# Where the weight sums of a Winograd feed-forward are made: in its first group, or by pieces in the stages before it

## The chip, the cores and the metric

The kernel runs on one core of a Trainium2 chip. The metric is the time of one execution on the device, in microseconds (us). Engines are named as the profile names them: PE is TensorE (with PEld, its weight loads), DVE is VectorE, ACT is ScalarE, POOL is GpSimd, SP is SyncE, which here only issues DMAs.

## What is computed

Two transformer layers over x of shape (2, 1024, 512) in float32. Each of four blocks is normed ahead and behind, and added to x:

```
x = x + ln(attention0(ln(x)))    # each token on its own: softmax of q.k over 8 heads of a group
x = x + ln(ffn0(ln(x)))          # ternary weights, hidden 1408, sigmoid gate
x = x + ln(attention1(ln(x)))    # 16 heads, 4 key/value heads, causal, rotary
x = x + ln(ffn1(ln(x)))          # hidden 2048
ffn1: h = silu(x @ w_gate) * (x @ w_up)
      of every 4 neighbours of h keep the 2 largest by size, the rest become 0
      return h @ w_down
```

The change concerns mostly `ffn1`, the last stage.

## The kernel before

The 2048 tokens are 16 tiles of 128, taken in 4 groups of 4 tiles; x stays in SBUF (`x_sb`). The stages follow each other: attention 0 with the loads, the first feed-forward (113 to 400 us, with the projections of the second attention's first tiles in its last group), the second attention (to 960 us), the last feed-forward (from 960.75 us).

**First feed-forward.** For each group and each of 11 hidden blocks `l0_hidden` (L365) multiplies (L371), gates, and splits the hidden tile in a rounded part and the rest; the rest is made on POOL (L380). `l0_out` (L385) multiplies both by the third weight two to three steps later (L390). A group's end adds the normed output to x on POOL (L411); the first block's output of the next group is added on POOL too (L300).

**Second attention.** It is a list of 96 steps (`t_steps`, L978), 16 tasks (batch, half of the queries, key head) in turn. A step (`prob_step`, L816) computes transposed scores for one block of keys, takes the exponential on ACT, and, on the diagonal, zeroes what lies ahead with `affine_select` on POOL (L838). `value_step` (L845) follows two steps later. Meanwhile `score_step` (L738) finds the row maxima (L758, DVE) and sums (L762, ACT) of later tasks, `shifts` (L796) turns them to logarithms on DVE, and a table `due` holds pieces of other work by step: `later` (L897) puts a function at a step. Through it go the projections of batch 1 (`project_parts`, L454: norm and transpose; project and rotate, with two adds on POOL at L520; transpose back, split and store to DRAM), the output tiles (`output_parts`, L862: multiply, norm, add to x on POOL at L876), and at the end the first work of the last stage (`f1_begin`, L1053).

**Last feed-forward.** Its products are made by Winograd's form of 2 x 2 block multiplication: seven products, for which each operand needs four sums of its blocks. A unit of weights (gate or up: eight units, two tiles each) has four raw blocks of 128 x 256 values, and the same in each of the four groups. `derive` (L927) makes the four sums on POOL, `load_unit` (L905) loads a unit two ahead. In group 0 a unit is loaded raw, derived, and its seven blocks' last four are kept in DRAM (`kept`); later groups load three raw blocks and four kept ones. Units 0 and 1 are derived within the attention, the others in group 0. The down weights (four parts `S`) go the same way (`load_down` L1116, `derive_down` L1130): parts 0 and 1 on POOL, 2 and 3 on DVE, the sums kept from group 0 on. A group has a hidden half (`f1_unit`, L1168, products at L1160, additions at L1166, gate products at L1221 and L1222, the choice of 2 of 4 at L1255 and L1280) and a down half (`f1_down`, L1305, products at L1315). `f1_collect` (L1321) adds the product sums of a pair of tiles, `f1_store` (L1359) norms them and adds them to x. The reciprocal root for the norm is made on DVE by 13 small operations (`inverse_root`, L182), save for the last pair, where ACT takes the square root (L177).

**Who sets the order.** `tc.manual_schedule(engines=...)` names the engines whose order is that of the program text. From L543 on and from L973 on that is PE alone; the order of DVE, ACT, POOL and SP is made by a planner with costs of its own. The last feed-forward (L1425) has all five engines in the order of the text. [...]

Of the kernel before, what the change touches and what calls it, by code (L numbers as in the profile page):

```python
# [18 lines left out]
P = 128  # L19
GT = 4  # L20
# [4 lines left out]
def two_layer_sandwich(  # L25
# [386 lines left out]


    NH, NKV, DK = 16, 4, 32
    REP = NH // NKV
# [33 lines left out]
    def a1_stats(st, G):  # L449
        tiles = [x_sb[:, st.b * TB + G * GT + k, :] for k in range(GT)]  # L450
        mv, rs = ln_stats(aw, tiles, f"a1_{st.b}_{G}", roots=False)
        st.ln[G] = mv, rs, minus_mean(aw, mv, rs, GT)

    def project_parts(st, i, on_act=False):  # L454
# [30 lines left out]
        def second():  # L485
# [20 lines left out]
            for h0, n, ps_qk, ct, sit, rb_h in (  # L506
                (NH, NKV, pkv, cos_t, sin_t, rbs[0]), (0, NH, pq, cosq_t, sinq_t, rbs[1])
            ):
                src = ps_qk[:, : n * DK].rearrange("p (h f) -> p h f", f=DK)
                ra_h = h.ra[:, h0 : h0 + n, :]  # L510
                nc.vector.tensor_tensor(
                    ra_h, src, ct[:, i, :].unsqueeze(1).to_broadcast([P, n, DK]), ALU.mult
                )
                half = [P, n, DK // 2]
                for par in range(2):
                    nc.vector.tensor_tensor(
                        rb_h[:, :, par::2], src[:, :, 1 - par :: 2],
                        sit[:, i, par::2].unsqueeze(1).to_broadcast(half), ALU.mult,
                    )
                nc.gpsimd.tensor_tensor(ra_h, ra_h, rb_h, ALU.add)  # L520

        def third():
            pq, pk = bank[0](f"pqT_{nm}"), bank[0](f"pkT_{nm}")
            ra = h.ra.rearrange("p h f -> p (h f)")
# [17 lines left out]

    with tc.manual_schedule(engines={mybir.EngineType.PE}):  # L543
        l0_stats(0, range(1))
# [67 lines left out]
        for g in range(NG):  # L612
            nxt = None
            for hc in range(HC):
# [28 lines left out]
                else:  # L643
# [5 lines left out]
                    if 1 <= hc <= 2 * GT:  # L649
                        if hc % 2:  # L650
                            parts[hc // 2][0]()
                            if hc > 1:
                                parts[hc // 2 - 1][2]()
                        else:
                            parts[hc // 2 - 1][1]()
                    elif hc == 2 * GT + 1:
                        parts[GT - 1][2]()
                        done[0] = GT
                        parts[GT][0]()
                if g == NG - 2 and hc == 4:  # L660
                    p0_stack.close()
# [200 lines left out]
    def output_parts(st, Q):  # L862

        def part(ii):
# [10 lines left out]
            ln_apply(tmp, py, mv, rs, 0)  # L875
            nc.gpsimd.tensor_tensor(xt, xt, tmp, ALU.add)  # L876

        return [lambda ii=ii: part(ii) for ii in range(GT)]

    P5_BUFS = 1  # L880
    dw = ctx.enter_context(
        tc.tile_pool(name="dw", bufs=FF // P, space=bass.MemoryType.DRAM)
    )

# [16 lines left out]
    w1a = None  # L901
    NU = FF // (2 * P)
    raw, derived, kept = {}, {}, {}

    def load_unit(n):  # L905


        res = []
        for i, src in enumerate((f1_wg, f1_wu)):
            pool = w1b if n % 3 == 2 else w1a  # L910
            w = pool.tile(
                [P, 7, 2, P], F32, tag="w7", name=f"w7_{n}_{i}", bufs=2 if n % 3 == 2 else 4
            )
            if n < NU:
                nc.sync.dma_start(out=w[:, 0:4].rearrange("p b c m -> p (b c m)"), in_=src[n])
            else:
                nc.sync.dma_start(
                    out=w[:, 0:3].rearrange("p b c m -> p (b c m)"), in_=src[n % NU][:, : 6 * P]
                )
                nc.sync.dma_start(out=w[:, 3:7], in_=kept[n % NU, i])  # L920
            res.append(w)
        if n < NU:
            raw[n] = res
        else:
            derived[n] = [[w[:, k] for k in range(7)] for w in res]

    def derive(n):  # L927

        res = raw.pop(n)
        for i, w in enumerate(res):
            a11, a12, a22, a21, s1_, s2_, s4_ = (w[:, k] for k in range(7))
            nc.gpsimd.tensor_tensor(s1_, a21, a22, ALU.add)
            nc.gpsimd.tensor_tensor(s2_, s1_, a11, ALU.subtract)
            nc.gpsimd.tensor_tensor(a21, a11, a21, ALU.subtract)
            nc.gpsimd.tensor_tensor(s4_, a12, s2_, ALU.subtract)
            kept[n, i] = dw.tile([P, 4, 2, P], F32, tag="kept", name=f"kept_{n}_{i}")
            nc.gpsimd.dma_start(out=kept[n, i], in_=w[:, 3:7])
        derived[n] = [[w[:, k] for k in range(7)] for w in res]  # L940

    HW = GW // 2

# [28 lines left out]

    with tc.manual_schedule(engines={mybir.EngineType.PE}):  # L973
        s_steps = [
# [64 lines left out]
        for b, i, at in begins:  # L1039
# [9 lines left out]

            later(at, [begin, lambda hold=hold: hold[1](), end])  # L1050
        f1_first = Task()
# [23 lines left out]
        later(len(t_steps) - 3 * GT * NQ, [f1_begin])  # L1075
        for n in range(2):
            later(len(t_steps) - 2 * GT * NQ + 4 * n, [lambda n=n: derive(n)])
        for k in range(GT):
# [10 lines left out]

        for step, (tk, j) in enumerate(t_steps):  # L1090
            prob_step(tk, j)
            prev.append((tk, j))

# [11 lines left out]
        while due:  # L1105
            step = min(due)
            for f in due.pop(step):
                f()
    at_stack.close()


    w1b = ctx.enter_context(tc.tile_pool(name="w1b", bufs=1))
    s2 = ctx.enter_context(tc.tile_pool(name="s2", bufs=2))
    down, raw_down, kept_down = {}, {}, {}

    def load_down(g, S):  # L1116


        w = w1b.tile([P, 7, 2, HW], F32, tag="wd7", name=f"wd7_{g}_{S}", bufs=2)
        if g == 0:  # L1120
            nc.sync.dma_start(out=w[:, 0:4].rearrange("p b j d -> p (b j d)"), in_=f1_wd[S])
            raw_down[S] = w
        else:
            nc.sync.dma_start(
                out=w[:, 0:3].rearrange("p b j d -> p (b j d)"), in_=f1_wd[S][:, : 3 * D]
            )
            nc.sync.dma_start(out=w[:, 3:7], in_=kept_down[S])
        down[g, S] = [w[:, k] for k in range(7)]

    def derive_down(S, eng):  # L1130


        w = raw_down.pop(S)
        b11, b21, b22, b12, t1, t2, t4 = (w[:, k] for k in range(7))
        eng.tensor_tensor(t1, b12, b11, ALU.subtract)
        eng.tensor_tensor(t2, b22, t1, ALU.subtract)
        eng.tensor_tensor(b12, b22, b12, ALU.subtract)
        eng.tensor_tensor(t4, b21, t2, ALU.subtract)
        kept_down[S] = dw.tile([P, 4, 2, HW], F32, tag="keptd", name=f"keptd_{S}", bufs=NS)
        nc.gpsimd.dma_start(out=kept_down[S], in_=w[:, 3:7])  # L1140

# [26 lines left out]
    def f1_unit(u, nm, B, w, h, ab, then):  # L1168
# [6 lines left out]
        gate = w1a.tile([P, 2, GW], F32, tag="gate", name=f"gate_{nm}", bufs=2)  # L1175
        p5 = w1a.tile([P, 2, HW], F32, tag="p5", name=f"p5_{nm}", bufs=P5_BUFS)
        hu = h.rearrange("p (i u) t -> p u i t", u=2)[:, u]
# [53 lines left out]
    def f1_hidden(g, S, B, then):  # L1231
# [5 lines left out]
        for u in range(2):  # L1237
            n = NU * g + 2 * S + u
            if n + 2 < NU * NG:
                load_unit(n + 2)  # L1240
            if n + 2 in raw:
                derive(n + 2)
            if S < 2 and u == 1:
                load_down(g, S)
            if g == 0 and S == NS - 1:
                derive_down(u, nc.gpsimd)
            f1_unit(u, f"{g}_{S}_{u}", B, derived.pop(n), h, ab, then)
# [73 lines left out]
    def f1_collect(nm, acc):  # L1321
# [19 lines left out]
        )  # L1341
        nc.vector.tensor_tensor(o[:, 1, :HW], acc[3][:, :HW], e[:, 1, :], ALU.add)
        return o

# [13 lines left out]

    def f1_store(g, k, o, late, final):  # L1359
        def add_x(i, mv, rs):  # L1360
# [9 lines left out]
        if final:  # L1370
            mv, rs = ln_stats(s2, [o[:, i, :] for i in range(2)], f"f1_{g}_{k}")
            nb = minus_mean(s2, mv, rs, 2)
            nc.scalar.activation(
                o[:, 1, :], o[:, 1, :], AF.Identity, scale=rs[:, 1:2], bias=nb[:, 1:2]
            )
            ln_apply(o[:, 0, :], o[:, 0, :], mv, rs, 0)
            for i, eng, queue in ((0, nc.vector, nc.sync), (1, nc.gpsimd, nc.gpsimd)):
                t = GT * g + k + 2 * i
                eng.tensor_tensor(x_sb[:, t, :], x_sb[:, t, :], o[:, i, :], ALU.add)
                queue.dma_start(out=of[:, t, :], in_=x_sb[:, t, :])  # L1380
            return

        items = norm_items([o[:, i, :] for i in range(2)], f"f1_{g}_{k}", use)
        if late:
            fill(items, 4)
        else:
            run(items)
# [37 lines left out]
    with tc.manual_schedule(engines={E.PE, E.Activation, E.DVE, E.SP, E.Pool}):  # L1425
        for g in range(NG):
# [28 lines left out]
            for S in range(NS):  # L1455
                if S >= 2:
                    run(token_sums(g, S, hs[S]))
                    if g == 0:
                        derive_down(S, nc.vector)
                for k in range(2):  # L1460
# [82 lines left out]
```

## Time and profile before

| | |
|---|---|
| median of 3 runs | 1573.17 us (1571.08 to 1573.36) |
| profiled execution | 1573.54 us, its span 1571.8 us |
| PE busy | 1473.6 us, 94% |
| DVE busy | 1027.6 us, 65% |
| ACT busy | 742.2 us, 47% |
| POOL busy | 317.7 us, 20% |
| load of a raw gate or up tile (512 KB) | lands after 3.7 to 6.1 us |
| store of four kept blocks (512 KB) | lands after 4.5 us |

All times in profile lines are us from the start of the span. A group's line names the source line, engine, operation, what is written and read with its shapes, the count, busy time and mean duration in ns, then the idle time ahead of it and what ended it. A line in order of time begins with its start and duration. "A <- B: total, times, longest" is the time that A's engine stood idle until B was done.

### The profile page before, as it was taken

The page shows a single profiled execution, that of the slowest core. Times are in us where ns is not written, and L with a number is a line of the kernel's source. Part 1 is how long each engine was busy: PE and PEld are TensorE (multiplying, and loading weights), DVE is VectorE, ACT ScalarE, POOL GpSimd, SP SyncE. Part 2 cuts the span into 40 slices and gives each one's busy share as a digit, 9 for nine tenths or more (in the row PEclk, how much of TensorE's full clock was granted, in tenths as well). Part 3 has the DMA queues.
Part 4 walks back from the last instruction along what each step waited for, and adds up shares of the span by engine and source line. Part 5 has one row for each costly group of instructions (what it writes and reads, how often), then busy time and mean ns, then how long its engine had stood idle before and what let it go on. Part 6 is the DMA issues. An engine that isn't in the chain of part 4 may idle for free.

```text
span 1571.8 us, 20347 instructions
## 1 busy us (share of the span) xinstructions
PE 1473.6 (94%) x6998; PEld 1054.4 (67%) x6998; DVE 1027.6 (65%) x2393; ACT 742.2 (47%) x1877; POOL 317.7 (20%) x392
## 2 busy tenths in 40 slices
PE   6999999999689999998889999989999999999996
PEld 3557787877445444444444446868888888888886
DVE  5886356433576677657767645898568568846783
ACT  4243344222287767796696982432145134404430
POOL 1112245232201211104212014850200010001001
PEclk9999999999869999998899999989999999999999
DMA  7200001111552312224220003552463345235411
GB/s 288 74 1 0 1 1 40 15 34 34 131 127 68 88 44 61 61 55 131 58 55 1 1 1 102 206 194 89 145 249 141 141 152 203 94 141 189 167 47 74
DMA packets 68767, 145.50 MB, mean 93 GB/s; under 512 B 9332, under 2 KB 30838, under 8 KB 66104
## 3 DMA queue, kind: packets, MB, share of 16 engines
q1 hardware_dynamic: 63528, 126.38, 25.5%
q0 software_dynamic: 4080, 16.52, 2.7%
q10 hardware_dynamic: 1056, 1.31, 0.3%
q8 instruction: 55, 0.90, 0.2%
q14 instruction: 48, 0.39, 0.1%
HBM read 116.92 MB, written 27.26 MB: 92 GB/s over the span
## 4 chain that ended last, share of the span: by engine, by line
PE 73%; DVE 13%; ACT 8%; issue 3%; POOL 1%; DMA 1%; SPq 0%; POOLq 0%; ACTq 0%; DVEq 0%
PE acc L1315 12%; PE ph L371 9%; PE pb_g L1160 6%; PE pb_u L1160 6%; ACT junk L762 5%; PE po L390 5%; PE psc L747 3%; PE pq L488 3%; PE pq L248 3%; PE pst L823 3%; PE po L852 3%; PE pc_g L1160 3%; PE pc_u L1160 3%; PE py L868 3%; DVE mxs L758 3%
## 5 line engine op out<-in xcount | busy, mean ns | idle before, releaser
L758 DVE TENSOR_REDUCE mxs<-psc 128x1 f32<-128x512 f32 (+3 forms) x384 | 196.4, 551 | 90.7 <-PE psc L753 50.5
L762 ACT ACTIVATE junk<-psc,mxs 128x512 bf16<-128x512 f32 (+3 forms) x384 | 223.2, 642 | 31.0 <-DVE mxs L758 20.1
L836 ACT ACTIVATE pT<-pst 128x512 f32<-128x512 f32 (+3 forms) x384 | 161.2, 563 | 54.2 <-PE pst L830 54.0
L371 PE MATMUL ph<-xTg,w 128*128 128x512 f32 x704 | 168.7, 393 | 3.0 <-DVE h L377 1.4
L747 PE MATMUL psc<-k,q 128*128 128x512 f32 (+3 forms) x384 | 146.5, 454 | 17.8 <-ACT junk L762 10.9
L371 PEld LDWEIGHTS ph<-xTg,w 128*128 128x128 f32 x704 | 131.2, 188 | 30.9 <-DVE h L377 1.8
L823 PE MATMUL pst<-q,k 128*128 128x512 f32 (+3 forms) x384 | 123.1, 410 | 12.1 <-ACT junk L762 10.4
L747 PEld LDWEIGHTS psc<-k,q 128*128 128x128 f32 x384 | 77.5, 212 | 81.9 <-ACT pT L836 31.8
L1315 PE MATMUL acc<-wd,h 128*128 128x256 f32 x512 | 121.6, 379 | 0.0
L838 POOL TENSOR_SCALAR_AFFINE_SELECT pT<-pT 128x256 f32<-128x256 f32 x128 | 52.1, 414 | 297.5 <-ACT pT L836 295.5
L823 PEld LDWEIGHTS pst<-q,k 128*128 128x128 f32 x384 | 67.6, 194 | 58.8 <-ACT junk L762 35.8
L1315 PEld LDWEIGHTS acc<-wd,h 128*128 128x128 f32 x512 | 97.0, 190 | 13.1
L1363 POOL TENSOR_TENSOR x_sb<-x_sb,o 128x512 f32<-128x512 f32 x14 | 19.2, 1374 | 427.2 <-DVE o L199 427.1
L762 ACT ACTIVATION_READ_ACCUMULATOR junk<-psc,mxs 128x1 f32 x384 | 101.9, 266 | 0.0
L852 PE MATMUL po<-pT,v 128*32 128x512 f32 (+3 forms) x768 | 92.7, 519 | 1.6 <-POOL pT L838 1.1
L1315 PE MATMUL acc<-wd,hx 128*128 128x256 f32 x384 | 93.3, 379 | 0.0
L377 DVE TENSOR_TENSOR h<-h,ph 128x512 f32<-128x512 f32 x44 | 30.0, 684 | 96.1 <-PE ph L371 95.1
L380 POOL TENSOR_TENSOR hl<-h,hl 128x512 fp32r<-128x512 f32 x44 | 57.3, 1303 | 169.0 <-ACT hl L379 169.0
L390 PE MATMUL po<-w,hl 128*128 128x512 f32 x352 | 87.4, 391 | 1.9 <-DVE tmp L199 1.9
L1315 PEld LDWEIGHTS acc<-wd,hx 128*128 128x128 f32 x384 | 73.0, 190 | 9.9
L1332 ACT COPY p<-acc 128x512 f32<-128x512 f32 x8 | 4.7, 586 | 157.7 <-PE acc L1315 157.7
L390 PEld LDWEIGHTS po<-w,hl 128*128 128x128 f32 x352 | 65.8, 188 | 17.0 <-DVE tmp L199 3.6
(276 smaller groups left out, 2897.4 us busy)
## 6 DMA issues: line engine op xcount, KB each, us to landing
w<-kept SPq DMA_DIRECT2D x48, 512.0 KB, 6.3
q<-dq SPq DMA_DIRECT2D x64, 256.0 KB, 4.8
wd<-keptd SPq DMA_DIRECT2D x12, 1024.0 KB, 9.5
dq<-hl SPq DMA_DIRECT2D x32, 320.0 KB, 3.1
w<-in_f_wg SPq DMA_DIRECT2D x24, 384.0 KB, 3.3
w<-in_f_wu SPq DMA_DIRECT2D x24, 384.0 KB, 5.7
wd<-in_f_wd SPq DMA_DIRECT2D x12, 768.0 KB, 6.8
kept<-w POOLq DMA_DIRECT2D x16, 512.0 KB, 4.5
```

Source lines behind the costliest of these rows:

```text
L371: nc.tensor.matmul(pa, wt[:, c, cols], xT[:, s, c, :], start=(c == 0 and s == 0), stop=(c == DC - 1 and s == 1),)
L380: nc.gpsimd.tensor_tensor(hl[:, 1, :], h, hl[:, 0, :].bitcast(F32), ALU.subtract)
L390: nc.tensor.matmul(pos0[g][k], hl[:, s, k * P : (k + 1) * P], w3[:, hc, :], start=(hc == 0 and s == 0), stop=(hc == HC - 1 and s == 1),)
L747: nc.tensor.matmul(pa[:, :w], tk.q.bitcast(F32R)[:, r, ii * P : (ii + 1) * P], st.k[ch].bitcast(F32R)[:, g, :w], start=True, stop=True,)
L758: nc.vector.tensor_reduce(mx, pa[:, :w], AX.X, ALU.max, negate=True)
L762: nc.scalar.activation(junk[:, :w], pa[:, :w], AF.Exp, bias=mx, accum_out=tk.sm[:, ii, r, ch : ch + 1])
L823: nc.tensor.matmul(pas[r][:, c0:], st.k[j // GT].bitcast(F32R)[:, g, (j % GT) * P : (j % GT + 1) * P], tk.q.bitcast(F32R)[:, r, c0:], star ...
L836: nc.scalar.activation(p[:, e, c0:], pas[2 * pr + e][:, c0:], AF.Exp)
L838: nc.gpsimd.affine_select(out=p[:, :, c0 : c0 + P], in_=p[:, :, c0 : c0 + P], compare_op=ALU.is_ge, fill=0.0, base=0, pattern=[[0, 2], [1, ...
L852: nc.tensor.matmul(tk.po[DK * r : DK * r + DK, c0:], st.v[j // GT][:, j % GT, g * DK : (g + 1) * DK], tk.pT[j, r // 2][:, r % 2, c0:], sta ...
L1160: nc.tensor.matmul(p, a[:, c, :], b[:, c, :], start=(first and c == 0), stop=(c == 1), skip_group_check=not first,)
L1315: nc.tensor.matmul(acc[m // 2][:, m % 2 * HW : (m % 2 + 1) * HW], a[:, j, k * P : (k + 1) * P], b[:, j, :], start=start, stop=True, skip_g ...
```

## The change

1. The sums of all weights are made before the last stage, in 24 pieces, and all groups (0 too) load three raw blocks and four kept ones. A piece is one gate or up tile (16) or half a down part (8): a load of 512 KB by SP, four POOL operations on 128 x 256 values, a store of 512 KB issued by POOL.
2. Eight pieces lie in the first feed-forward: begun (loaded) at hidden steps 0, 3, ..., 21, in the memory of the first attention's query weight; ended (four operations and store together) two steps later.
3. Sixteen pieces lie in the second attention: piece k is loaded at step 2 + 4k into one of two buffers of a new pool, and its four operations come one by one at steps 4 + 4k to 7 + 4k, the store behind the fourth.
4. In the first feed-forward and the attention POOL's order is now that of the program text, as PE's.
5. Within the attention, POOL's adds for the rotation and for the outputs are held until behind the next step's `prob_step`; the third part of a batch 1 projection comes one step later.
6. In the last group the first pair takes its root on ACT; the last pair's two tiles are normed one after the other. The first is scaled on ACT and added on POOL; the last part of the second (`finish_o`) is summed behind that, scaled and added on DVE.

The core of the diff:

```diff
+    def left_piece(pool, tag, bufs, n, i):
+        w = pool.tile([P, 8, 2, P], F32, tag=tag, name=f"wl_{n}_{i}", bufs=bufs)
+        nc.sync.dma_start(
+            out=w[:, 0:4].rearrange("p b c m -> p (b c m)"), in_=(f1_wg, f1_wu)[i][n]
+        )
+        kept[n, i] = dw.tile([P, 4, 2, P], F32, tag="kept", name=f"kept_{n}_{i}")
+        a11, a12, a22, a21, s1_, s2_, s4_ = (w[:, k] for k in range(7))
+        return kept[n, i], w, (
+            (s1_, a21, a22, ALU.add), (s2_, s1_, a11, ALU.subtract),
+            (a21, a11, a21, ALU.subtract), (s4_, a12, s2_, ALU.subtract),
+        )
...
+    def begin_piece(pool, tag, bufs):
+        f, a, b = pieces.pop(0)
+        begun.append(f(pool, tag, bufs, a, b))
+
+    def end_piece(k=None):
+        if begun:
+            to, w, ops = begun[0]
+            for op in ops if k is None else ops[k : k + 1]:
+                nc.gpsimd.tensor_tensor(*op)
+            if k is None or k == 3:
+                nc.gpsimd.dma_start(out=to, in_=w[:, 3:7])
+                begun.pop(0)
...
+    def soon(f):
+        if hold_adds[0]:
+            waiting_adds.append(f)
+        else:
+            f()
...
-                nc.gpsimd.tensor_tensor(ra_h, ra_h, rb_h, ALU.add)
+                soon(lambda a=ra_h, b=rb_h: nc.gpsimd.tensor_tensor(a, a, b, ALU.add))
...
-    with tc.manual_schedule(engines={mybir.EngineType.PE}):
+    with tc.manual_schedule(engines={mybir.EngineType.PE, mybir.EngineType.Pool}):
...
+                step = HC * g + hc
+                if step <= HC * (NG - 2) + 3:
+                    if step % 3 == 2:
+                        end_piece()
+                    elif step % 3 == 0 and step < HC * (NG - 2) + 2:
+                        begin_piece(p0, "wq0", 1)
...
-            nc.gpsimd.tensor_tensor(xt, xt, tmp, ALU.add)
+            soon(lambda: nc.gpsimd.tensor_tensor(xt, xt, tmp, ALU.add))
...
-            later(at, [begin, lambda hold=hold: hold[1](), end])
+            later(at, [begin, lambda hold=hold: hold[1](), flush, end])
+        for k in range(len(pieces)):
+            later(2 + 4 * k, [lambda: begin_piece(tw, "w8", 2)])
+            for i in range(4):
+                later(4 + 4 * k + i, [lambda i=i: end_piece(i)])
...
-        for n in range(2):
-            later(len(t_steps) - 2 * GT * NQ + 4 * n, [lambda n=n: derive(n)])
...
+            hold_adds[0] = True
             prob_step(tk, j)
+            flush()
...
-            if n + 2 in raw:
-                derive(n + 2)
...
-            if g == 0 and S == NS - 1:
-                derive_down(u, nc.gpsimd)
...
+            for i in range(2):
                 t = GT * g + k + 2 * i
+                mv, rs = ln_stats(s2, [o[:, i, :]], f"f1_{g}_{k}_{i}")
+                if i == 0:
+                    nb = minus_mean(s2, mv, rs, 1)
+                    nc.scalar.activation(
+                        o[:, 0, :], o[:, 0, :], AF.Identity, scale=rs[:, 0:1], bias=nb[:, 0:1]
+                    )
+                    finish_o()
+                    eng, queue = nc.gpsimd, nc.gpsimd
+                else:
+                    ln_apply(o[:, 1, :], o[:, 1, :], mv, rs, 0)
+                    eng, queue = nc.vector, nc.sync
                 eng.tensor_tensor(x_sb[:, t, :], x_sb[:, t, :], o[:, i, :], ALU.add)
                 queue.dma_start(out=of[:, t, :], in_=x_sb[:, t, :])
...
+        elif g == NG - 1:
+            use(*ln_stats(s2, [o[:, i, :] for i in range(2)], f"f1_{g}_{k}"))
```

## The prediction

> **What bounds the kernel now.** I read first the engines' busy times stage by stage, for the last feed-forward, whose four groups do the same work. Columns: stretch and length, then PE, PEld, DVE, ACT and POOL busy with counts, PE clock, DMA share, GB/s. These are the hidden halves of groups 0, 1 and 2:
>
> ```profile
> 960.75:1071.10 110.35, 102.42 (x450) 88.04 (x449) 91.45 (x148) 45.80 (x98) 69.11 (x72) 0.95 0.53 186
> 1121.19:1218.05 96.86, 96.86 (x451) 85.23 (x450) 74.56 (x149) 44.55 (x97) 7.51 (x8) 1.00 0.51 182
> 1267.90:1364.84 96.94, 96.94 (x452) 85.29 (x451) 74.64 (x149) 44.63 (x97) 7.58 (x8) 1.00 0.51 182
> ```
>
> PE never stops in groups 1 and 2. Group 0 takes 13.45 us longer; DVE does the same number of instructions in 17 us more, and POOL is busy 69 us, not 7.5. Next PE's waits in group 0 (in groups 1 and 2 there are none), and the two stalls in order of time:
>
> ```profile
> PE pc_g L1160 <- DVE gate L1166: 3.5, 1, 3.5
> PE pb_g L1160 <- ACT gate L1208: 2.4, 1, 2.4
> PE pb_g L1160 <- DVE gate L1166: 2.0, 2, 1.8
> ...
> 1040.34 2.05 PE L1160 MATMUL pc_g<-xdg,w 128*128 128x256 f32 x4 [3.52 <-DVE gate L1166]
> 1042.18 1.91 PE L1160 MATMUL pb_u<-xTg,w 128*128 128x256 f32 x4
> ...
> 1055.49 1.13 PE L1160 MATMUL pb_g<-xdg,w 128*128 128x256 f32 x4 [2.42 <-ACT gate L1208]
> 1056.46 1.72 PE L1160 MATMUL pb_u<-xdg,w 128*128 128x256 f32 x4
> 1057.97 1.91 PE L1160 MATMUL pb_g<-xTg,w 128*128 128x256 f32 x4
> ```
>
> 7.9 us is idle; the rest is matmuls started 1.7 us apart, not 0.86, behind a gap. Then why DVE is late, by its groups in group 0 and then in group 1:
>
> ```profile
> L1222 DVE TENSOR_TENSOR h<-h,gate 128x1024 f32<-128x1024 f32 x7 | 10.6, 1516 | 0.2
> L1166 DVE TENSOR_TENSOR h<-h,pc_u 128x256 f32<-128x256 f32 x8 | 3.3, 413 | 1.9 <-PE pc_u L1160 1.8
> ...
> L1222 DVE TENSOR_TENSOR h<-h,gate 128x1024 f32<-128x1024 f32 x7 | 8.6, 1225 | 0.2
> L1166 DVE TENSOR_TENSOR h<-h,pc_u 128x256 f32<-128x256 f32 x8 | 3.3, 416 | 2.1 <-PE pc_u L1160 2.1
> ```
>
> The product of two SBUF tiles stretches beside POOL (1516 against 1225 ns); the addition fed from PSUM does not (413, 416). Last, the attention (430 to 960 us), in order of time where units 0 and 1 are derived now:
>
> ```profile
> 745.48 2.86 DVE L789 SCALAR_TENSOR_TENSOR lgp<-lgp,lgy 128x16 f32<-128x16 f32 x1
> ...
> 750.33 0.58 PE L747 MATMUL psc<-k,q 128*128 128x256 f32 x1 [4.84 <-ACT junk L762]
> ...
> 751.72 5.92 PE L868 MATMUL py<-wc,oT 128*128 128x512 f32 x8
> ```
>
> An operation of 0.16 us is held until POOL's run of back-to-back work ends at 748.29, PE stops 4.84 us, and the projection behind it takes 5.92 us, not 3.65.
>
> **1. Group 0 loses its derivations.** Gone there: 12 gate/up tiles x 4 POOL operations, the down sums (8 operations on POOL, 8 on DVE) and 16 stores. POOL keeps only the four adds of the attention's end, so DVE should run as in group 1: 110.35 - 96.9 = -13.4 us. Group 0 now loads kept sums too: its traffic becomes that of group 1, where 182 GB/s at share 0.51 makes no PE wait, so 0. The down half was full already (50.09 of 50.09): 0. Here the Trainium skill ("TensorE: Matmul & The Clock Gate", Part 1) halves the clock only after an idle window of about 3.4 us. By it only the 3.52 us gap would slow the matmuls: 7.9 idle + 3.1 slow = 11.0 us to win. The row behind the 2.42 us gap shows 1.91 us per four all the same, another 1.8 us. I take the measured 13.4; ends 11.0 and 14.
>
> **2. The clump in the attention goes.** 16 operations (0.73 us each) and 4 stores leave 727 to 749 us. Stretched DVE operations there exceed their usual 0.16 us by some 7.5 us; PE lost 1.67 + 4.84 idle and 2.3 in the slow projection: 8.8 us. Against 824 to 859 us, which holds the same four output tiles (PE busy 33.5 of 35), 735 to 770 shows 27.3 at clock 0.80. I take -8; ends -3 (the output norms fall there anyway) and -11.
>
> **3. Twenty-four pieces are added.** Each is 4 x 0.73 + 0.57 us for the store's descriptors + 0.3 us wait = 3.8 us of POOL.
>
> Eight lie in the first feed-forward, one per three hidden steps of 5.44 us. POOL is 30 to 39% busy there, and the matmuls that consume its `hl` run two to three steps behind, so its 3.8 us hide; PE's waits there total 4.3 us. Load, four operations and store need about 5 + 3.5 + 4.5 = 13 us of 16.3. Uncovered, a late `hl` would cost up to 3.8 us. I take +1; ends 0 and +4.
>
> Sixteen lie in the attention, one operation per step, 47 us of POOL. POOL is 20% busy, so its own time is hidden; DVE's is the price. The skill speaks against this move ("GPSIMD Engine Reference", Key points): GpSimd shares its SBUF interfaces with VectorE, which suffers with two SBUF inputs or in a two-port mode, so contention is moved, not removed. Were all 47 us to collide, they would eat the gain twice over. The rows say what is exposed: the score maxima (L758, 181 us) read PSUM and took 0.68 us beside POOL's sums at 734 to 737, as elsewhere; the small SBUF operations (roots, logarithm, casts; their rows sum to about 85 us) are 16% of 525 us, and dense in perhaps a quarter of the steps. 47 x 0.16 to 47 x 0.25 = 7.5 to 11.7 us of DVE delay. A lone operation holds DVE 0.73 us, too short for a slow clock, and DVE is rarely PE's last wait, so I pass on half: +5; ends 0 and +12.
>
> **4. POOL's order fixed.** Behind a waiting sum stand the next step's `affine_select`s, for which PE's value matmuls wait (1.1 us now); also for adds, hence these are held until after the selects. A tile's rotation and its third part come one step (5 us) later; no task needs them until scores several steps on: 0. In the first feed-forward the four adds of L300 (5.7 us) and a piece now stand in text order ahead of a later `hl`, which the two to three steps of lag (11 us) cover; its price is in the +4 above. POOL's store queue gets 24 stores for 20. SP gets 16 loads and later eight instead of four unit loads, 0.43 us each: it idles far longer. The other engines' new planned order is unknown: 0; ends -4 and +4.
>
> **5. The tail.** Order of time before:
>
> ```profile
> 1556.50 0.17 DVE L188 TENSOR_SCALAR nv_f<-mv_f 128x2 f32<-128x2 f32 x1
> ...
> 1560.58 0.69 DVE L1336 TENSOR_TENSOR e<-acc,o 128x512 f32<-128x512 f32 x1
> ...
> 1567.27 0.56 POOL L1380 DMA_DIRECT2D out<-x_sb  x1 [0.30 <-POOL x_sb L1379]
> ```
>
> The second-last pair trades 13 small DVE operations (1556.5 to 1558.85) for a square root (0.30) and a reciprocal (0.17), so `e` of the last pair starts when its matmul ends: 6.05 us (one block of 28 matmuls) behind that of the pair before (1553.10), 1559.15, 1.4 us sooner. From there by the rows of before: `e` and `o` 1.4, statistics of the first tile 0.87, root, reciprocal and bias 0.8, ACT's scaling 0.81, POOL's add 1.31 and a wait of 0.3: its store is issued at 1564.7. The second tile: its last part 0.42 from 1562.2, statistics 0.9, root 0.4, reciprocal 0.2, scaling 0.54, DVE's add 0.69: SP's store at 1565.5, now the last, 1.8 us before 1567.27. POOL's add for the pair before (1.3 us) may hold DVE's two-input sum by some tenths. I take -1.5; ends -0.5 and -2.2.
>
> **Sum.** -13.4 - 8 + 1 + 5 + 0 - 1.5 = -16.9 us. Against the profiled execution (span 1571.8, time 1573.54) this gives 1556.6; the runs' median is 0.37 lower: 1556.
>
> **The rivals.**
> - The attention gives the bubble back (0.20): PE follows every DVE delay, +11.7 for +5, and the planner's order adds 1: about -9, 1564. For it: in the clump PE lost all that DVE lost. Against: there the operations ran back to back.
> - Group 0 is not POOL's doing (0.05): its first pass would still stall, leaving -8 + 1 + 5 - 1.5 = -3.5: 1570, no change to be told. Against: groups 1 and 2 do the same on DVE without a wait.
> - Slower (0.07): a piece's load stands on SP behind a `q` load that waits for its buffer (up to 34 us, 12 times 199 us in SP's waits), its first sum holds POOL, the selects and PE's values. It decides from 17 / 16 = 1.1 us per piece on; with half the pieces 4 us late, 32 - 17 = +15: 1588. Against: two steps (about 10 us) between load and sum, and a load of this size lands in 3.7 to 6.1 us.
> - The forecast (0.68): 1549 to 1564 by its bounds.
>
> The range, 1548 to 1567, takes in the first rival and leaves out the other two and some of each edge. A measurement can tell 0.2% (3.1 us) from no change: faster 0.88, same 0.05, slower 0.07.
>
> **What would show it.** Group 0's hidden half at 96 to 98 us with no PE wait and L1222 near 1225 ns (step 1); no PE gap over 2 us between the output tiles of batch 0 (2); POOL some 35 us busier from 430 to 960 us, L758 unchanged, PE's waits on DVE and ACT there grown by 5 us at most (3); `po<-POOL pT` still near 1 us (4); the last `out` issued near 1565.5 less what came before (5). Wrong if PE waits for POOL in the attention, or if group 0 still stalls.

## The result and the profile after

The changed kernel takes 1551.88 us (median of 4 runs, 1551.75 to 1552.05) beside 1572.12 us before on the same chip (4 runs, 1567.08 to 1573.36): a ratio of 0.9877, interval 0.9855 to 0.99. It is faster by 20 us, where 17 were predicted (a time of 1556). The profiled execution's span is 1550.0 us against 1571.8.

Where the 21.8 us of the two spans come from, by stages (us; the first feed-forward from its first `ph` matmul to its last `po` matmul, the attention from there to the last stage's first product; "last" is the down half of group 3 with the tail):

```
                    to 1st ffn  1st ffn  attention  g0 hidden  g0 down  g1..g3 hidden  last    span
before                113.91    288.68     558.16     110.35     50.09      390.27     60.34  1571.8
after                 113.84    292.35     547.40      96.69     50.10      390.27     59.35  1550.0
difference             -0.1      +3.7      -10.8      -13.7       0          0         -1.0    -21.8
predicted                        +1         -3        -13.4       0          0         -1.5    -16.9
```

Group 0 of the last feed-forward first. Its hidden half and that of group 1, in the profile after, by busy times (columns as in the prediction's first view):

```profile
953.59:1050.28 96.69, 96.69 (x450) 85.07 (x448) 70.60 (x148) 45.82 (x98) 2.54 (x2) 1.00 0.53 191
1100.38:1197.07 96.69, 96.69 (x450) 85.07 (x448) 74.38 (x149) 44.58 (x97) 7.51 (x8) 1.00 0.50 183
```

Group 0 is now like the others: PE is busy for all of 96.69 us at full clock, and POOL only 2.54 us. What had made DVE late has gone with it; its groups in group 0, after (L1258 and L1202 are L1222 and L1166 of before):

```profile
L1258 DVE TENSOR_TENSOR h<-h,gate 128x1024 f32<-128x1024 f32 x7 | 8.6, 1225 | 0.2
L1202 DVE TENSOR_TENSOR h<-h,pc_u 128x256 f32<-128x256 f32 x8 | 3.4, 419 | 3.0 <-PE pc_u L1196 3.0
```

The product of two SBUF tiles takes 1225 ns instead of 1516. DVE now waits for PE's `pc_u`, and PE for nothing.

In the attention I followed the last `affine_select` of each of the 16 tasks. After minus before, these ends stand at +5.4, +3.3, +1.8, +3.4, +1.9, +1.9, +2.5 and +3.0 us for the first eight tasks, at -2.7 for the ninth, at -5.6 for the next three, and at -6.2 to -7.2 for the last four. So 8.5 of the stage's 10.8 us arise between the ends of the eighth and the tenth task (717 to 778 us before), where the clump of derivations and the slow projection behind it stood. PE's longest waits around it, in the profile after (700 to 780 us):

```profile
PE pst L898 <- ACT junk L837: 4.0, 7, 1.0
PE psc L822 <- ACT junk L837: 2.0, 1, 2.0
PE pst L905 <- ACT mT L795: 1.2, 1, 1.2
```

The 4.84 us gap is gone, the longest left is 2.0 us. The pieces themselves, on POOL in order of time, after (a line begins with start and duration; the bracket is the idle time ahead and what ended it):

```profile
521.48 0.95 POOL L913 TENSOR_SCALAR_AFFINE_SELECT pT<-pT 128x256 f32<-128x256 f32 x2 [2.73 <-ACT pT L911]
522.41 0.72 POOL L463 TENSOR_TENSOR wl<-wl 128x256 f32<-128x256 f32 x1
525.76 0.77 POOL L913 TENSOR_SCALAR_AFFINE_SELECT pT<-pT 128x256 f32<-128x256 f32 x2 [2.63 <-ACT pT L911]
526.49 0.72 POOL L463 TENSOR_TENSOR wl<-wl 128x256 f32<-128x256 f32 x1
```

One sum of 0.72 us stands behind a step's selects and is done 2.6 us before POOL is wanted again. DVE's score maxima did not change with it (before 196.4 us, mean 551 ns; they read PSUM); they are L833 in the page after:

```profile
L833 DVE TENSOR_REDUCE mxs<-psc 128x1 f32<-128x512 f32 (+3 forms) x384 | 196.1, 551 | 88.8 <-PE psc L828 48.7
```

The first feed-forward lost 3.7 us. By the starts of its 44 hidden steps on PE it stands 2.6 us ahead of before at the start of the 29th and 3.7 behind at that of the 32nd, so 6.3 us are lost at one place, behind the last piece. PE, DVE and POOL there, after, in order of time:

```profile
286.06 3.20 PE L371 MATMUL ph<-xTg,w 128*128 128x512 f32 x8 [2.55 <-DVE h L377]
```
```profile
259.99 8.59 DVE L199 TENSOR_SCALAR ao<-ao,mv_ao,rs_ao 128x512 f32<-128x512 f32 x4
...
285.31 0.69 DVE L377 TENSOR_TENSOR h<-h,ph 128x512 f32<-128x512 f32 x1
```
```profile
252.89 5.06 POOL L411 TENSOR_TENSOR x_sb<-x_sb,tmp 128x512 f32<-128x512 f32 x4 [4.44 <-DVE tmp L199]
257.89 3.24 POOL L463 TENSOR_TENSOR wl<-wl 128x256 f32<-128x256 f32 x4
262.02 2.55 POOL L380 TENSOR_TENSOR hl<-h,hl 128x512 fp32r<-128x512 f32 x2
264.52 3.77 POOL L300 TENSOR_TENSOR x_sb<-x_sb,ao 128x512 f32<-128x512 f32 x3
```

From 252.89 us on POOL works with no pause over 0.4 us: the adds of the group's end, the piece, `hl`, the adds of L300. DVE's four scalings of `ao` beside it took 8.59 us; before, with no piece there, they took less than half of that:

```profile
262.69 3.88 DVE L199 TENSOR_SCALAR ao<-ao,mv_ao,rs_ao 128x512 f32<-128x512 f32 x4
```

DVE's planned order has the statistics of the new x, which need L300, ahead of the `h` that PE needs, and DVE is busy without a break from 259.99 to that `h` at 285.31. PE stands 2.55 us and runs slowly behind the gap (eight matmuls in 3.20 us, at a granted clock of 0.50 from 286.9 to 290.1 us).

The tail after, DVE, POOL and SP's queue merged in order of time:

```profile
1538.33 0.69 DVE L1368 TENSOR_TENSOR e<-acc,o 128x512 f32<-128x512 f32 x1 [0.51 <-PE acc L1347]
1539.06 2.00 DVE L1371 TENSOR_TENSOR o<-e,p 128x512 f32<-128x512 f32 x1
1539.22 1.27 POOL L1400 TENSOR_TENSOR x_sb<-x_sb,o 128x512 f32<-128x512 f32 x1
...
1545.27 0.56 POOL L1423 DMA_DIRECT2D out<-x_sb  x1 [0.30 <-POOL x_sb L1422]
1546.01 0.34 SPq L1423 DMA_DIRECT2D out<-x_sb  x1
```

`e` starts when its matmul ends, as planned. But the sum behind it (L1371, two SBUF inputs) takes 2.00 us beside POOL's add for the pair before; at 1533.01 us, with no POOL add beside it, the same line took 0.69.

### The profile page after: what moved, and what is told of

Its sections match the earlier page's. It is cut to its first block, busy times and chain, and to the rows that moved or that the text cites. A ratio compares the mean times of both kernels' runs of the same rounds, so it can differ in the third digit from the quotient of the medians.

```text
span 1550.0 us, 20371 instructions
## 1 busy us (share of the span) xinstructions
PE 1464.6 (94%) x6998; PEld 1050.3 (68%) x6998; DVE 1002.7 (65%) x2374; ACT 742.8 (48%) x1879; POOL 316.1 (20%) x420
## 3 DMA queue, kind: packets, MB, share of 16 engines
q10 hardware_dynamic: 1056, 1.31, 0.3%
## 4 chain that ended last, share of the span: by engine, by line
PE 76%; ACT 9%; DVE 9%; issue 3%; POOL 2%; DMA 0%; ACTq 0%; DVEq 0%; SPq 0%; POOLq 0%
PE acc L1347 12%; PE ph L371 7%; PE pb_u L1196 7%; PE pb_g L1196 7%; ACT junk L837 6%; PE po L390 4%; PE pq L248 4%; PE pq L556 4%; PE pc_g L1196 4%; PE pc_u L1196 4%; PE py L943 3%; PE po L927 3%; PE pst L898 3%; PE psc L822 3%; DVE mxs L833 3%
## 5 line engine op out<-in xcount | busy, mean ns | idle before, releaser
L833 DVE TENSOR_REDUCE mxs<-psc 128x1 f32<-128x512 f32 (+3 forms) x384 | 196.1, 551 | 88.8 <-PE psc L828 48.7
L822 PE MATMUL psc<-k,q 128*128 128x512 f32 (+3 forms) x384 | 142.5, 444 | 12.4 <-ACT junk L837 7.8
L837 ACT ACTIVATION_READ_ACCUMULATOR junk<-psc,mxs 128x1 f32 x384 | 98.6, 257 | 0.0
L1257 DVE TENSOR_TENSOR gate<-gate,ab 128x1024 f32<-128x1024 f32 x32 | 39.2, 1225 | 58.9 <-ACT ab L1254 58.9
```

What stands on the lines that cost most here:

```text
L822: nc.tensor.matmul(pa[:, :w], tk.q.bitcast(F32R)[:, r, ii * P : (ii + 1) * P], st.k[ch].bitcast(F32R)[:, g, :w], start=True, stop=True,)
L833: nc.vector.tensor_reduce(mx, pa[:, :w], AX.X, ALU.max, negate=True)
L837: nc.scalar.activation(junk[:, :w], pa[:, :w], AF.Exp, bias=mx, accum_out=tk.sm[:, ii, r, ch : ch + 1])
```

## The experiments

All times are medians of 4 to 17 runs, with a ratio to the kernel before on the same chip and its interval. Runs of one kernel spread by several us (before: 1566 to 1576), so two of these kernels whose intervals overlap are not told apart by their times alone. The stages come from one profile each. Six kernels (after, `g0_pool_back`, `ffn_nosums`, `shift_and_tail` and the two with piece 22) have the same order of instructions on PE, DVE, ACT and POOL through the attention, and it took 544.8 to 551.1 us in them, 548.9 in the mean: a difference of 3 us in that stage is not told from none. The first feed-forward varies by some 1.6 us, the stretch ahead of it by 2, the others by a tenth, save group 0's hidden half where POOL works in it. The stages of every run (before and after are in the table above):

```
                    to 1st ffn  1st ffn  attention  g0 hidden  g0 down  g1..g3 hidden  last    span
g0_pool_back          114.14    292.28     551.07     107.67     50.10      390.27     59.37  1564.9
att_clump             113.79    292.36     550.36      96.69     50.10      390.27     59.43  1553.0
bef_noclump           111.97    288.56     547.97     111.68     50.10      390.27     60.35  1560.9
bef_order             113.98    285.02     558.45     108.31     50.09      390.27     60.38  1566.5
att_nosums            113.56    293.89     545.33      96.69     50.10      390.27     59.36  1549.2
ffn_nosums            113.55    285.78     550.98      96.70     50.09      390.27     59.33  1546.7
pool_planned          114.11    297.49     566.04      96.69     50.10      390.27     59.40  1574.1
shift_and_tail        114.01    289.37     550.14      96.70     50.09      390.28     59.31  1549.9
piece22_psum_tail     112.56    286.29     548.90      96.70     50.09      390.28     58.08  1542.9
piece22_split         113.87    287.41     544.81      96.70     50.09      390.27     58.05  1541.2
```

**Was group 0 POOL's doing?** The kernel after, with POOL's work put back into group 0, where it was, on a tile that nobody reads:

```diff
+    if g == 0 and n + 2 < NU:
+        for b7 in derived[n + 2]:
+            for _ in range(4):
+                nc.gpsimd.tensor_tensor(scrap[:, :, :P], b7[1], b7[2], ALU.add)
+    if g == 0 and S == NS - 1:
+        for _ in range(4):
+            nc.gpsimd.tensor_tensor(scrap, down[g, u][0], down[g, u][1], ALU.add)
```

> The changed kernel with 48 POOL operations (two SBUF inputs, 128 x 256) and 8 of 128 x 512 put back into group 0's hidden half, where the derivations stood. They write to a tile that nobody reads, so no engine waits for their result; only POOL's presence beside DVE returns. Theory (POOL's run of work holds and stretches DVE): the hidden half goes from 96.7 to 107 to 112 us, L1222's product (L1258 here or near it) from 1225 to 1450 ns or more, time 1562 to 1567. Rival (PE waited for the derived weights or their loads): the half stays at 97 to 98 us, time 1552 to 1553.

Measured: 1566.26 us, ratio 0.9958 (0.9946 to 0.9971). Group 0's hidden half, its busy times, two of its DVE groups and all of PE's waits in it:

```profile
957.50:1065.20 107.70, 100.97 (x450) 86.93 (x449) 88.84 (x148) 45.82 (x98) 65.98 (x58) 0.95 0.47 171
```
```profile
L1258 DVE TENSOR_TENSOR h<-h,gate 128x1024 f32<-128x1024 f32 x7 | 10.6, 1516 | 0.2
L1202 DVE TENSOR_TENSOR h<-h,pc_u 128x256 f32<-128x256 f32 x8 | 3.3, 414 | 2.3 <-PE pc_u L1196 2.3
```
```profile
PE pb_g L1196 <- DVE gate L1202: 3.4, 2, 2.3
PE pc_g L1196 <- DVE gate L1202: 3.3, 1, 3.3
```

Nothing waits for this work, yet 11.0 of the 13.7 us come back, as the theory had it, with the same stretched product (1516 ns) and PE's waits for DVE's `gate` (3.3 and 3.4 us; before: 3.5 and 2.0). It is POOL's presence beside DVE, not a wait for the sums. The other 2.7 us may lie in what was not put back (the stores, the dependence on the derived blocks, 3 us of POOL's time) or in the stage's own spread: in the three kernels that derive there it takes 108.3 to 111.7 us.

**Does spreading matter, or only leaving the clump's place?** After, with a piece's four sums in one step:

```diff
-            for i in range(4):
-                later(4 + 4 * k + i, [lambda i=i: end_piece(i)])
+            later(7 + 4 * k, [end_piece])
```

> The changed kernel with each attention piece's four sums and store issued together at step 7 + 4k instead of one sum a step; the same 64 operations. Theory (the length of POOL's run makes the price, a lone 0.73 us operation is absorbed): a run of 2.9 us and more holds DVE; the attention lengthens by 4 to 15 us, time 1556 to 1567. Rival (only the sum of POOL's time counts): within 2 us of 1552.

Measured: 1555.36 us, 0.9893 (0.9868 to 0.9919). That is 3.5 us more than after, 3.0 of them in the attention (550.36), just short of what the theory asked for. The intervals overlap and 550.36 lies among the six kernels with spread sums, so a price of runs of four is not shown; if there is one, it is far below the some 8 us of the one clump of sixteen.

**The clump alone.** The kernel before, with the sums of units 0 and 1 left out (raw blocks stand in their place):

```diff
-    derive: four nc.gpsimd.tensor_tensor per tile
+    derive: the same, if n >= 2
+    load_unit: for n < 2 three more raw blocks of each tile, into the place of sums
```

> The kernel before with the 16 POOL sums of units 0 and 1 within the attention left out (units 0 and 1 use raw blocks in place of sums; their loads and stores stay, plus four loads of 384 KB). Group 0's own derivations stay. Theory (the clump alone made the attention's bubble): the stretch from the eighth to the ninth task's end shrinks by 8 to 10 us, time 1561 to 1565. Rival (the output norms of these steps make the bubble, or POOL's fixed order cured it): less than 3 us, time 1569 to 1573.

Measured: 1564.58 us, 0.9949 (0.9931 to 0.9968), 8.9 less than before on that chip. The attention takes 547.97 us, 10.2 less than before. The time is as the theory had it. The stretch that it named, from the eighth to the ninth task's end, shrinks by 4.2 us, and up to the tenth by 7.0; 2.6 more had come before the clump, which is within the stage's spread. The clump is worth 7 to 9 us.

**POOL's order alone.** The kernel before, with both stages' POOL in the order of the text and the held adds, and no pieces:

```diff
-    with tc.manual_schedule(engines={mybir.EngineType.PE}):
+    with tc.manual_schedule(engines={mybir.EngineType.PE, mybir.EngineType.Pool}):
...
+    soon(...), flush() and the extra step of later(at, ...), as in the change
```

> The kernel before with POOL's order fixed as in the text, adds held behind the next step's selects, and the third part of a projection one step later, nothing else: derivations stay where they were. Theory (fixed order is worth nothing by itself; the clump stays a clump): 1569 to 1575. Rival (the order gives the attention's gain): 1560 to 1565, the bubble gone.

Measured: 1567.87 us, 0.9975 (0.996 to 0.9989), a little below what the theory allowed. The first feed-forward is 3.66 us shorter. PE's longest waits in it, before:

```profile
PE po L390 <- DVE tmp L199: 1.9, 4, 0.5
PE ph L371 <- DVE h L377: 1.4, 1, 1.4
```

and with POOL's order fixed:

```profile
PE ph L371 <- DVE xTg L361: 0.7, 1, 0.7
...
PE po L390 <- DVE tmp L199: 0.6, 2, 0.3
```

The wait for `h` is gone, that for `tmp` is 0.6 instead of 1.9 us (all of PE's waits there: 5.8 us before, 3.0 here). Around 255 us the planner's order had an `hl` ahead of a group's four adds (L411), for which DVE's `tmp` waits; the order of the text has them ahead of it.

The attention takes as long as before (558.45), but that is the sum of two changes. At the end of the 14th task, counted from the end of the first feed-forward, it stands 8.1 us ahead of before: the bubble between 717 and 778 us is gone, because the 16 sums no longer lie there. The planner had put them at 727 to 749 us; in the order of the text they come at 883 to 916, and the selects stand behind them. There the last two tasks lose 8.4 us:

```profile
909.19 0.73 POOL L948 TENSOR_TENSOR w<-w 128x256 f32<-128x256 f32 x1
...
916.78 1.47 POOL L852 TENSOR_SCALAR_AFFINE_SELECT pT<-pT 128x256 f32<-128x256 f32 x4
```
```profile
917.25 1.85 PE L866 MATMUL po<-pT,v 128*32 128x384 f32 x8 [6.04 <-POOL pT L852]
```

The selects could not pass the eight sums and two stores ahead of them in POOL's order, and PE waited 6.04 us for them. So the same sums cost some 8 us by what they did to DVE at one place and some 8 us by POOL's own turn at another; that the two are alike is chance.

**What the sums in the attention cost.** After, with the attention's 64 sums left out (loads and stores stay; the first four blocks are stored as they came):

```diff
-                nc.gpsimd.tensor_tensor(*op)
+                if k is None: nc.gpsimd.tensor_tensor(*op)
```

> The changed kernel with the 64 POOL sums of the sixteen attention pieces left out (raw blocks are stored in their place; loads and stores stay). It prices the spread sums. Forecast of record (half of DVE's delay passes to PE): 5 us less, 1546 to 1548. Theory now (lone operations are absorbed): 0 to 2 us less, 1550 to 1552.

Measured: 1550.79 us, 0.9865 (0.985 to 0.988). The attention takes 545.33 us, 2.1 less than after and 3.6 less than the mean of the six; the medians differ by 1.1, as the later theory had it. So the 64 spread sums cost 1 to 4 us, which is no more than the stage's own spread.

**What the sums in the first feed-forward cost.** The same with the other eight pieces' 32 sums left out (`if k is not None`).

> The changed kernel with the 32 POOL sums of the eight pieces in the first feed-forward left out (raw blocks stored; loads and stores stay). Theory (the first feed-forward is 3.7 us longer because POOL's run of L411's adds, a piece and L300's adds held DVE's scaling of the attention output near 260 us): the first feed-forward comes back to 288 to 290 us, time 1548 to 1549. Rival (the order of POOL's adds, L300 behind hl, does it without the sums): still 291 us or more, time 1551 to 1552.

Measured: 1546.17 us, 0.9835 (0.9814 to 0.9856). The first feed-forward takes 285.78 us, 6.6 less than after (medians: 5.7), more than the theory asked for. By the starts of the hidden steps 1.1 us of this is lost near the piece at step 8 and 5.5 near the last one; the other six pieces cost nothing.

**The pieces without the order.** After, with POOL in the planner's hands again:

```diff
-    with tc.manual_schedule(engines={mybir.EngineType.PE, mybir.EngineType.Pool}):
+    with tc.manual_schedule(engines={mybir.EngineType.PE}):
```

> The changed kernel with POOL's order given back to the planner in the first feed-forward and the attention; pieces, held adds and tail stay. Theory (what counts is that the sums are apart; the planner's order lets sums bunch up and adds stand in front): 0 to 8 us longer, 1552 to 1560. Rival (the fixed order itself is a brake, since what waits on POOL holds what is behind): 1548 to 1551.

Measured: 1570.75 us, 0.9998 (0.9983 to 1.0013), far above both forecasts. All is lost again. POOL in order of time in the attention of this kernel:

```profile
504.66 2.89 POOL L463 TENSOR_TENSOR wl<-wl 128x256 f32<-128x256 f32 x4
507.84 0.58 POOL L465 DMA_DIRECT2D kept<-wl  x1 [0.30 <-POOL wl L463]
508.44 2.93 POOL L463 TENSOR_TENSOR wl<-wl 128x256 f32<-128x256 f32 x4
511.67 0.57 POOL L465 DMA_DIRECT2D kept<-wl  x1 [0.30 <-POOL wl L463]
512.25 0.77 POOL L913 TENSOR_SCALAR_AFFINE_SELECT pT<-pT 128x256 f32<-128x256 f32 x2
```

The planner runs all 16 pieces between 481 and 632 us, four or eight sums in a row, some ahead of the selects. The attention takes 566.04 us, 18.6 more than after, and nearly all of it is lost by the end of the fifth task. PE's longest wait between 480 and 640 us is for DVE's norm of an output tile, and the same wait in the profile after (475 to 635 us) is shorter:

```profile
PE psc L822 <- DVE tmpy L199: 4.9, 1, 4.9
```
```profile
PE psc L822 <- DVE tmpy L199: 1.3, 1, 1.3
```

This is the way of the old clump, through DVE. Runs of four did no such harm at fixed steps (550.36), so the length of a run is not what decides; which of the planner's choices does was not separated. The first feed-forward takes 5.1 us more than after; there PE waits for POOL itself:

```profile
PE po L390 <- POOL hl L380: 4.0, 2, 2.5
```

**The stall near 285 us and the tail.** After, with the last piece of the first feed-forward one step later, and the second-last pair's second tile added on DVE and stored by SP:

```diff
-                    if step % 3 == 2:
+                    if step == 24 or step % 3 == 2 and step != 23:
...
+    last group, pair 0: add_x(0, ...); tile 1: ln_apply, nc.vector.tensor_tensor, nc.sync.dma_start
```

> The changed kernel with two repairs: the last piece of the first feed-forward is summed one hidden step later (step 24, not 23, so it isn't between L411's adds and the next hl), and in the last group the first pair's second tile is added on DVE and stored by SP, so that no POOL add runs beside DVE's two-input sum of the last pair (2.00 us there instead of 0.69). Theory: first feed-forward 289 to 290 us (2 to 3.5 less), tail 0.8 to 1.2 us less, time 1547.5 to 1549.5. Rival (the delay at 260 us comes from L300 behind hl, whichever piece stands near): first feed-forward unchanged, time 1550.5 to 1551.

Measured: 1548.74 us, 0.985 (0.9831 to 0.9869). The time and the first feed-forward (289.37) came out as forecast, but not in the way that was forecast. PE's stall, in order of time, is still there:

```profile
284.82 2.11 PE L371 MATMUL ph<-xTg,w 128*128 128x512 f32 x8 [2.52 <-DVE h L377]
```

DVE's scaling of `ao` fell to 3.22 us, and its planned order now had one `h` ahead of the statistics of the new x; but the piece still stood ahead of L300, for which DVE waits before later `h`. And DVE's new add in the tail was held in its turn, beside POOL's for the other tile:

```profile
1537.19 1.64 DVE L1435 TENSOR_TENSOR x_sb<-x_sb,o 128x512 f32<-128x512 f32 x1
```

The tail kept its length (59.31), where 0.8 to 1.2 us less were forecast. The hold had only moved to another sum of two SBUF inputs.

**Both again, by what was learned.** The last piece one step earlier, where POOL stands idle for 4.4 us, and the tail's sum with one input straight from PSUM:

```diff
-                    if step % 3 == 2:
+                    if step == 22 or step % 3 == 2 and step != 23:
...
-            o[:, :, HW:], e, p15[:, 1:2, :].to_broadcast(two), ALU.add
+            o[:, :, HW:], e, halves(acc[0])[:, 1:2, :].to_broadcast(two), ALU.add
```

> The changed kernel with two other repairs. The last piece of the first feed-forward is summed at step 22 (not 23), ahead of the L411 adds, where POOL has waited 4.4 us for DVE. And the last pair's two-input sum on DVE takes its second operand from the PSUM bank, not from its SBUF copy. Theory (the stall near 285 us is DVE waiting, in its planned order, for the x sums of L300, which any piece between L411 and L300 delays; and POOL holds DVE only where both operands are in SBUF): no PE gap near 285 us, first feed-forward 287 to 289.5 us; that sum takes 0.7 us beside POOL's add, not 2.00, and the stretch from the last down half's start to the end is 58.0 to 58.4 us, not 59.35; time 1545 to 1548.5. Rival (POOL's sum of work is what counts there; the hold does not depend on where the operand lies): first feed-forward 291 us or more, the sum still 1.3 us or more, time 1550.5 to 1552.

Measured: 1546.24 us, 0.9841 (0.9818 to 0.9865). The stall is gone, and the first feed-forward takes 286.29 us: 6.1 less than after, so nearly the whole price of the eight pieces was the place of this one. DVE's order in that stage is the one of the run just above, so 3.1 us of it are the piece's place ahead of L300 alone. The tail is 1.27 us shorter than after. DVE and POOL in the tail, in order of time:

```profile
1533.22 0.69 DVE L1371 TENSOR_TENSOR o<-e,acc 128x512 f32<-128x512 f32 x1
```
```profile
1533.39 1.28 POOL L1400 TENSOR_TENSOR x_sb<-x_sb,o 128x512 f32<-128x512 f32 x1
```

POOL's add runs beside it as before, but the sum that reads PSUM takes 0.69, not 2.00 us. This version is below both kernels, by 5.6 us in its median against after; the intervals overlap a little, the profiles show where the gain lies.

**Should the first feed-forward's pieces be split too?** The same, with two sums of a piece ahead of `l0_hidden` and two behind:

```diff
-                        end_piece()
+                        end_piece(0); end_piece(1)
                     l0_hidden
+                        end_piece(2); end_piece(3)
```

> As the run with the last piece at step 22 and the PSUM operand, and each piece of the first feed-forward in two runs of two sums, one ahead of the step's own hl operation and one behind it. Theory (shorter runs hold DVE less): 0 to 2 us less in the first feed-forward than with runs of four, 1544 to 1548. Rival (runs of four are covered there once none stands ahead of L300): no difference beyond 0.5 us in the first feed-forward.

Measured: 1546.51 us, 0.9841 (0.9825 to 0.9857). The first feed-forward takes 287.41 us, 1.1 more than with runs of four (286.29), lost at the piece of step 8. Neither forecast came; spreading further wins nothing there.

## Why the prediction was right, and where its steps failed

The direction and the range held, and the two large terms, which were read from the profile of before, came in their mechanism and in their size. The small terms were less good and partly cancelled. The largest miss is the attention's net: -3 was forecast, -10.8 measured.

- **Step 1 (-13.4) held:** -13.7, with every sign that was named. Eleven of it is POOL's presence alone. That 11.0 is not the 11.0 that the prediction worked out from the idle window of the Trainium skill ("TensorE: Matmul & The Clock Gate", Part 1): with POOL's work put back POOL is 3 us less busy than before, and the alikeness is chance. Of the window the trace shows another thing: behind the 2.42 us gap, which is shorter, the granted clock was 0.50 as well (1056.7 to 1060.0 us before).
- **Step 2 (-8) held:** 8.5 us arise where the clump stood, 7.0 there with the clump alone left out, and 8.9 in the medians of that run.
- **Step 3, attention (+5):** mis-sized, as far as is known. The step is the half of DVE's delay that was to pass on to PE. The sums cost 1 to 4 us, and PE's waits for DVE in the stage fell from 8.0 to 5.3 us although POOL was busy for 139 instead of 98 us. With -8.5 for the clump and some +2 for the sums, about 4 us of the stage's -10.8 have no cause assigned; that is about what the stage varies by from run to run, so they stay open. (The 181 us that the prediction gives for the score maxima are 196 in the page; they did not matter.)
- **Step 3, first feed-forward (+1):** failed for one piece of eight. "So its 3.8 us hide" was argued from POOL's busy share and from the lag of `hl`. It is so for six pieces, at step 8 it is 1.1 us off, and the piece at step 23 made most of the 6.6 us that the 32 sums cost. PE never waited for `hl`. It waited for DVE: at step 23 POOL is not at its mean share but full, ahead of L300, which stands ahead of `h` in DVE's order. The lag covered one consumer; DVE was the other. (PE's waits in the stage of before were 5.8 us, not the 4.3 that the prediction gives.)
- **Step 4 (0):** failed. Alone, the order is worth -3.7 us in the first feed-forward, inside the end of -4, and in the attention it moves the clump from one cost of 8 us to another. With the pieces it decides everything: without it the gain is gone (1570.75 against 1551.88, 19 us). The prediction priced the order by what it delays, never by where the planner would put the pieces. The predicted place of the cost (L300 ahead of a later `hl`) was near the real one, but the one held was DVE.
- **Step 5 (-1.5):** -1.0. Its structure held; "some tenths" for the held sum were 1.3 us. The last store was due at 1565.5 less the 20.8 us that came before it, 1544.7; it was issued at 1546.01, later by that 1.3.

Steps 3 and 4 miss together: order and pieces make +3.7 us in the first feed-forward, since -3.7 and +6.6 stand against each other there (the other +0.8 was not assigned). That the total came within 5 us of the forecast is in part this cancelling.

The rivals did not come: the attention didn't give the bubble back (PE was to follow every DVE delay, +11.7 us; 1 to 4 came), group 0 was POOL's doing, and no piece's load held POOL, which waits for none of them in the profile after. The loss that the first rival feared does come, at 1571, in the kernel with the same sums in the planner's order.

## What to carry to other kernels

GpSimd work that nobody waits for can still have a price, and where it stands makes the price. Here 64 single sums between steps cost 1 to 4 us in all, while 16 sums in one clump cost 7 to 9, and with the planner's order for the 64 the stage lost 18.6. So move such work together with an order that keeps it in its place. Ask of each piece what stands behind it on its own engine and, one engine further, what waits for that in a fixed order; a mean busy share hides the one step in which the engine is full, and here one piece of eight made nearly the whole loss. A stage that is as long as before may hide a gain and a loss, so follow it in time. Where a sum of two SBUF tiles must run beside GpSimd, try one input from PSUM, which was not held here.

## What the runs showed of the hardware that was not expected

- A DVE sum of two SBUF tiles beside one POOL sum was stretched by about that sum's length: 2.00 us instead of 0.69 beside 1.27 us of POOL. With one input in PSUM it took 0.69 beside 1.28.
- The same hold met the DVE add that was meant to avoid it (1.64 us beside a POOL add of 1.42), so moving a sum between engines did not free it.
- Work on a tile that no instruction reads cost PE 11 us in one hidden half; all of PE's waits there were for DVE.
- PE's clock was granted at 0.50 for some 3.3 us behind gaps of only 2.42 us (before, near 1056 us) and 2.55 us (after, near 286 us).
